# Routing done batch by batch, and half of the shared expert dealt between routed experts, in a cross-attention and mixture-of-experts layer

## The chip, the cores and the metric

The kernel runs on one core of a Trainium2 chip. The metric is the device time of one execution in microseconds (us). Before the change three runs gave 1760.06 us in the median (1760.02 to 1762.03). Everything below about single instructions comes from one further execution, which was profiled.

The engines are named as in the profile: PE is the matrix engine and PEld its weight loads, DVE the vector engine, ACT the scalar engine, POOL the general engine that also issues indirect DMAs, SP the engine that issues most other DMAs. Each runs its instructions in order.

## The reference

A layer of cross-attention, then a mixture-of-experts layer, on `x` of 4 batches of 512 tokens with 512 features; the context has 1601 rows a batch, of which the first 257 are an image and have weights of their own.

```python
h = x + xattn(layernorm(x), ctx)       # 16 heads of 32; softmax over text rows plus softmax over image rows
n = layernorm(h).reshape(T, 512)       # T = 2048 tokens
scores = sigmoid(n @ router_w.T)       # 32 experts in 8 groups of 4
sc = scores + e_bias
group = sum of the two largest sc of each group; keep the 3 best groups
topk_idx = 4 largest of the kept sc    # topk_w = their scores, normalised to sum 2.5
# capacity: each expert takes the first 80 tokens (in token order) that chose it
Y[e] = (silu(X[e] @ W_gate[e]) * (X[e] @ W_up[e])) @ W_down[e]      # X[e]: up to 80 x 512; I = 256
out = scatter_add(Y * w) + (silu(n @ shared_gate.T) * (n @ shared_up.T)) @ shared_down.T
return h + out
```

So one part of the result (the shared expert, hidden size 512) is computed for every token, and another (the routed experts) for 32 lists of at most 80 tokens. Both are added to `h`.

## The kernel before

**Attention.** A loop over the four batches `b` (line 517). It first projects keys: four blocks of context rows times four chunks of features, 16 calls of `keys` (line 595 on), and between these calls, from a hand-written table `side` (line 578), it runs norms (`take_norms`, `take_normed`) and the largest scores of the first head group (`scores`, lines 286 to 292, four PE matmuls into four banks and four DVE reductions). A hand-written list (line 601) follows, with the rest of these, values, and `residual` of the batch before (lines 421 to 457: output projection, `x1`, layer norm `xn`, transposed `xnT`, router logits). Then come four chunks of heads `c`, each a loop over 13 tiles `t` of keys (line 642): scores of the next chunk (`wave`, DVE reductions), exponentials on ACT (`exps`), weighted sums on PE, and sums of the exponentials (`added`) on POOL, in the last chunk on DVE.

PSUM has eight banks, which `psum` (line 123) hands out in turn; a new tile in a bank waits until the bank's last reader is done. `Later` (line 86) holds work that becomes due after so many steps.

Large SBUF tiles of 128 x 4 x 512 come from one pool of five buffers, `wide` (line 134): exponentials, weights and later the shared expert's input and hidden layer. After the last batch the first `xT` is loaded (line 711).

**Shared expert and routing.** `shared` (line 837) makes 48 units of work for the four batches: for each batch four `gate` and four `up` units (hidden chunks) and four `down` units (token tiles). Each is four matmuls of 128 x 128 by 512 in the program. A batch's downs are dealt between the next batch's gates; the downs of batch 3 come last. A down fetches the tile of `x1` from `x1_d` through SP, adds on DVE and stores to `out` through SP (lines 868 to 876).

The loop at line 977 issues the units one by one. At fixed units (8 and on) it puts in the residual work of batch 3, and after each unit as many routing steps as a budget allows (`SHARE`, `spent`). Routing (line 728) is a chain of small DVE operations: selection (scores, groups, four rounds of maximum), then a write of the weights into `xw_d` next to the normalised tokens, then `ranks` (PE transposes) and the search, in which DVE finds the 80 best-ranked tokens of every expert eight at a time (`max`, `match_replace`). It runs twice: `first` for batches 0 to 2 (12 tiles of 128 tokens) and `second` for batch 3. Weights of the first four experts are loaded at units 10, 14, 18 and 22. When all routing is issued, `tokens` (line 828) turns the result into token indices, with a PE transpose, and POOL gathers the rows of the first four experts.

**Routed experts.** A loop of 33 rounds (line 1003). Round `e` projects gate and up of expert `e`, has POOL gather rows for `e + 4`, transposes the rows of `e + 2`, and does the down projection of `e - 1`: ACT scales it into `y` (three buffers), and POOL issues an indirect DMA that adds `y` into rows of `out` (line 925). Then SP issues the weights of expert `e + 3`, 1.5 MB, into one of four sets of buffers. Each of these DMAs to `out` waits for the one before to land.

Of the kernel before, what the change touches and what calls it, by code (L numbers as in the profile page):

```python
# [80 lines left out]


# [25 lines left out]
def body(ctx, tc, a, ident, mhalf, logits, x1_d, xw_d, xnT_d, den_d, rec_d, out):  # L108
# [9 lines left out]
    pt, hold, row, st = pool("pt", 5), pool("hold", 4), pool("row", 5), pool("st", 3)  # L118
# [15 lines left out]
    def wide(name):  # L134
        return pt.tile([P, NC, 512], F32, name=name, tag="wide")
# [285 lines left out]
    def residual(b, qt, aoT, wo):  # L421
# [9 lines left out]
        def project_o():  # L431
            ps = psum()
            project(ps, lambda k: aoT[:, k, qt * P:(qt + 1) * P], lambda k: wo()[:, k, :])
            t["x1"] = rowt("x1")
            nc.vector.tensor_tensor(t["x1"], ps, t["xr"], ALU.add)
            nc.sync.dma_start(x1_d[rows, :], t["x1"])
            t["moments"] = moments(t["x1"])
# [21 lines left out]
    def queries(b, xs, n):  # L459

        qT = kv.tile([P, NC, L], F32, name="qT", bufs=2)
        xlT = kv.tile([P, NC, L], F32, name="xlT")
# [8 lines left out]
        return qT, sq, turn, [partial(part, c, at) for c in range(NC) for at in range(0, L, n)]  # L471

# [42 lines left out]
    nc.vector.tensor_tensor(v_b, v_b, vi_b, ALU.add)  # L515
    pending = []
    for b in range(B):
# [16 lines left out]
        sqs, rs = {"q": sq_q}, {}  # L534

# [59 lines left out]
        for bl in range(NB):  # L595
            for c in range(NC):
                keys(bl, c)
                for f in side.get((bl, c), ()):
                    f()
                later.step()  # L600
# [10 lines left out]
        for c in range(NC):  # L611
# [30 lines left out]
            for t in range(NKT):  # L642
# [32 lines left out]
                while t and done * (NKT - 1) < len(fill) * t:  # L675
                    fill[done]()
                    done += 1
                later.step()
                if more and t == NKT - 1:
                    part = parts[(c + 1) % 2]  # L680
                    split(mx, part, NM)
                if prepares:
# [28 lines left out]
    first_xT = wide("xT")  # L711
    nc.sync.dma_start(first_xT, xnT_d[:, :, :L])
# [11 lines left out]
    NR = NT - NQ  # L724
    SHARE = 2.3
    AHEAD = 4

    def routing(lo, n):


        tt, ts, tr = nc.vector.tensor_tensor, nc.vector.tensor_scalar, nc.vector.tensor_reduce

        def full(name):
            return rp.tile([P, NR, E], F32, name=name, tag=name)[:, :n, :]

        def small(name, k=1):
            return rp.tile([P, NR, k], F32, name=name, tag=name)[:, :n, :]

        def groups(name):
            return rp.tile([P, NR, NG, NG], F32, name=name, tag=name)[:, :n]  # L740

        lg = logits[:, lo:lo + n, :]
        sc, sb, cand, hit, sel, chosen = (full(x) for x in ("sc", "sb", "cand", "hit", "sel", "chosen"))
        m = [small(f"m{i}", NG) for i in range(4)]
        gs, rank, top = small("gs", NG), small("rank", NG), small("top")
        gt, eq = groups("gt"), groups("eq")
        g = sb.rearrange("p t (g k) -> p t g k", k=EG)
        one = gs.unsqueeze(3).to_broadcast([P, n, NG, NG])
        oth = gs.unsqueeze(2).to_broadcast([P, n, NG, NG])
        rv = rev.to_broadcast([P, n, E])  # L750
        before = below.unsqueeze(1).to_broadcast([P, n, NG, NG])

        def wide_(x):
            return x.to_broadcast([P, n, E])

        work = [
            lambda: nc.scalar.activation(sc, lg, AF.Sigmoid),
            lambda: tt(sb, sc, e_b.unsqueeze(1).to_broadcast([P, n, E]), ALU.add),

            lambda: tt(m[0], g[:, :, :, 0], g[:, :, :, 1], ALU.max),  # L760
            lambda: tt(m[1], g[:, :, :, 0], g[:, :, :, 1], ALU.min),
            lambda: tt(m[2], g[:, :, :, 2], g[:, :, :, 3], ALU.max),
            lambda: tt(m[3], g[:, :, :, 2], g[:, :, :, 3], ALU.min),
            lambda: tt(m[1], m[1], m[3], ALU.max),
            lambda: tt(m[3], m[0], m[2], ALU.min),
            lambda: tt(m[0], m[0], m[2], ALU.max),
            lambda: tt(m[1], m[1], m[3], ALU.max),
            lambda: tt(gs, m[0], m[1], ALU.add),

            lambda: tt(gt, oth, one, ALU.is_gt),  # L770
            lambda: tt(eq, oth, one, ALU.is_equal),
            lambda: tt(eq, eq, before, ALU.mult),
            lambda: tt(gt, gt, eq, ALU.add),
            lambda: tr(rank, gt, AX.X, ALU.add),
            lambda: ts(rank, rank, float(TKG), None, ALU.is_lt),
            lambda: tt(
                cand.rearrange("p t (g k) -> p t g k", k=EG), g, rank.unsqueeze(3).to_broadcast([P, n, NG, EG]), ALU.mult
            ),
        ]

        for k in range(TOPK):
            into = sel if k else chosen
            work += [
                lambda: tr(top[:, :, 0], cand, AX.X, ALU.max),
                lambda: tt(hit, cand, wide_(top), ALU.is_equal),
                lambda: tt(hit, hit, rv, ALU.mult),
                lambda: tr(top[:, :, 0], hit, AX.X, ALU.max),
                lambda into=into: tt(into, hit, wide_(top), ALU.is_equal),
            ]
            if k:  # L790
                work.append(lambda: tt(chosen, chosen, sel, ALU.add))
            if k < TOPK - 1:
# [258 lines left out]
```

## Time and profile before

| what | value |
|---|---|
| median of three runs | 1760.06 us |
| profiled execution, whole / its span | 1755.5 / 1753.8 us |
| mean clock granted to PE | 0.992 |
| PE, DVE, ACT, POOL busy | 1699.4, 954.3, 642.4, 866.2 us |
| attention ends and the shared expert begins on PE | 1344 us |
| first expert transpose on PE | 1534.9 us |
| last `y` on ACT, last scatter on POOL | 1738.2, 1746.3 us |
| weights of one matrix of an expert, issue to landing | 5.3 to 7.0 us (512 KB) |
| scatter `out<-y`, on POOL / issue to landing | 1.42 / 5.7 us (3.7 to 8.1) |
| gather `xp<-xw_d`, on POOL / issue to landing | 0.93 / 5.4 us (2.8 to 7.6) |

The page is read from the slices inwards: they cut the span in 40 equal parts, each digit being the busy share of an engine in tenths. Matmul ends are modelled, so that a full PE may still hide short waits. A line of the order of time gives start, duration, engine, source line, operation and tiles; in brackets stands how long the engine was idle before it and what ended the wait. In a list of waits the numbers are total us, times, and the longest.

### The profile page before, as it was taken

To read this page: it belongs to the slowest core of one execution; us is meant where nothing else is said; L and a number is where in the kernel's file an instruction comes from. 1 tells how busy PE (TensorE), PEld (TensorE's weight loads), DVE (VectorE), ACT (ScalarE), POOL (GpSimd) and SP (SyncE) were. 2 spreads that over 40 slices of the span, in tenths; PEclk is the share of its full clock that TensorE was granted. 3 is DMA by queue.
4 is the path that set the end of the run, shared out by engine and by line. 5 is a ranking of instruction groups with operands and counts; after the bars stand their busy time and mean duration, and the time that the engine had idled before them with its cause. 6 is when DMAs were issued, how large, how long until landed. Compare 5 with 4: busy or idle time off the path is not lost. (4 is left out here: it accounts for less than half of the span.)

```text
span 1753.8 us, 29354 instructions
## 1 busy us (share of the span) xinstructions
PE 1699.4 (97%) x11825; PEld 895.0 (51%) x11825; DVE 954.3 (54%) x1861; ACT 642.4 (37%) x1368; POOL 866.2 (49%) x612
## 2 busy tenths in 40 slices
PE   6999999999999999999999999999999999998896
PEld 3564444456544444564444445644442454486674
DVE  3675554757555556665555648555557767411110
ACT  2125456611355565114555631245556010011111
POOL 2327878332569753328679432388782300123332
PEclk9999999999999999999999999999999999999998
DMA  6000000311100004020000040300011453379994
GB/s 226 1 2 1 26 22 6 110 65 56 42 1 26 26 13 150 19 79 13 27 1 27 14 161 13 108 2 14 14 49 63 144 185 114 97 262 292 294 288 102
DMA packets 68455, 138.38 MB, mean 79 GB/s; under 512 B 16096, under 2 KB 28512, under 8 KB 66144
## 3 DMA queue, kind: packets, MB, share of 16 engines
q1 hardware_dynamic: 59984, 125.42, 21.0%
q0 software_dynamic: 5120, 10.82, 3.1%
q8 instruction: 93, 1.52, 0.4%
q10 hardware_dynamic: 3216, 0.28, 0.1%
q14 instruction: 42, 0.34, 0.1%
HBM read 113.68 MB, written 22.81 MB: 78 GB/s over the span
## 5 line engine op out<-in xcount | busy, mean ns | idle before, releaser
L356 ACT ACTIVATE pT<-ps 128x512 f32<-128x512 f32 (+1 forms) x832 | 429.4, 604 | 344.0 <-PE ps L355 333.6
L318 DVE TENSOR_REDUCE mx<-ps 128x1 f32<-128x512 f32 (+1 forms) x576 | 331.3, 617 | 289.0 <-PE ps L304 289.0
L371 POOL TENSOR_TENSOR acc<-acc,pT 128x1024 f32<-128x1024 f32 x192 | 445.6, 2363 | 3.0 <-ACT pT L356 2.7
L363 PE MATMUL po<-pT,v 128*32 128x512 f32 (+2 forms) x1792 | 222.2, 603 | 0.0
L274 PEld LDWEIGHTS ps<-v_w,cT 128*128 128x128 f32 (+1 forms) x1408 | 168.9, 186 | 102.2 <-DVE mx L318 56.1
L355 PE MATMUL ps<-qT,kT 32*128 32x512 f32 (+1 forms) x1664 | 214.0, 587 | 0.0
L304 PE MATMUL ps<-kT,qT 32*128 32x512 f32 (+1 forms) x1536 | 205.2, 549 | 0.0
L274 PE MATMUL ps<-v_w,cT 128*128 128x128 f32 (+1 forms) x1408 | 197.7, 284 | 0.0
L213 PE MATMUL ps<-cT,wk 128*128 128x512 f32 (+1 forms) x384 | 153.9, 546 | 0.0
L292 DVE TENSOR_REDUCE mx<-ps 128x1 f32<-128x512 f32 (+2 forms) x256 | 128.4, 566 | 7.2 <-PE ps L289 7.2
L925 POOL DMA_INDIRECT out<-y,tok x32 | 45.4, 1419 | 140.8 <-DMA out<-y,tok 73.7
L220 POOL TENSOR_TENSOR sq_k<-sq_k,sq 128x512 f32<-128x512 f32 (+2 forms) x48 | 49.5, 1031 | 115.0 <-ACT sq L217 115.0
L352 PEld LDWEIGHTS <-pick 32*128 32x128 bf16 (+1 forms) x832 | 21.6, 91 | 165.7 <-issue 164.0
L213 PEld LDWEIGHTS ps<-cT,wk 128*128 128x128 f32 x384 | 69.6, 190 | 70.5 <-issue 54.3
L282 ACT COPY v<-ps 128x128 f32<-128x128 f32 (+1 forms) x208 | 60.1, 289 | 118.4 <-PE ps L274 117.8
L378 POOL TENSOR_TENSOR acc<-pT 128x1024 f32<-128x1024 f32 x24 | 56.1, 2359 | 86.7 <-ACT pT L356 54.1
L371 DVE TENSOR_TENSOR acc<-acc,pT 128x1024 f32<-128x1024 f32 (+1 forms) x72 | 97.8, 1405 | 2.1 <-ACT pT L356 2.1
L915 DVE TENSOR_TENSOR ehT<-ehT,ps 128x160 f32<-128x160 f32 x32 | 10.3, 321 | 162.0 <-ACT ehT L914 162.0
L371 POOL TENSOR_TENSOR pT<-pT 65x1024 f32<-65x1024 f32 x24 | 56.0, 2349 | 85.8 <-PE po L363 77.3
L304 PEld LDWEIGHTS ps<-kT,qT 32*128 32x128 f32 x1536 | 81.0, 183 | 30.8 <-issue 10.1
L363 PEld LDWEIGHTS po<-pT,v 128*32 128x32 f32 (+2 forms) x1792 | 34.7, 107 | 118.8 <-issue 109.3
L890 POOL DMA_INDIRECT xp<-xw_d,tok x32 | 30.0, 937 | 120.3 <-DVE tok L835 110.8
(178 smaller groups left out, 2233.8 us busy)
## 6 DMA issues: line engine op xcount, KB each, us to landing
W_gate<-in_W_gate SPq DMA_DIRECT2D x32, 512.0 KB, 5.6
W_up<-in_W_up SPq DMA_DIRECT2D x32, 512.0 KB, 7.0
W_down<-in_W_down SPq DMA_DIRECT2D x32, 512.0 KB, 5.3
xt<-in_x SPq DMA_DIRECT2D x32, 256.0 KB, 3.5
cT<-in_ctxT SPq DMA_DIRECT2D x8, 1024.0 KB, 9.4
rb<-rec_d SPq DMA_DIRECT2D x64, 128.0 KB, 2.7
wk<-in_k_w SPq DMA_DIRECT2D x4, 1024.0 KB
wki<-in_k_img_w SPq DMA_DIRECT2D x4, 1024.0 KB, 10.5
```

What stands on the lines that cost most here:

```text
L213: nc.tensor.matmul(ps[:, :n], lhsT=wt[:, k, c * P:(c + 1) * P], rhs=xT[:, k, to], start=k == 0, stop=k == NC - 1)
L220: nc.gpsimd.tensor_tensor(sq[:, to], sq[:, to], s, ALU.add)
L274: nc.tensor.matmul(ps[lo:hi, :], lhsT=cTs[bl][:, k, at:at + hi - lo], rhs=ws[bl == NB - 1][:, k, c * P:(c + 1) * P], start=k == 0, stop=k ...
L282: nc.scalar.copy(v[:n, t, :], ps[:n])
L292: nc.vector.tensor_reduce(mx[:, qt, g, bl:bl + 1], ps[:, :n], AX.X, ALU.max, negate=True)
L304: nc.tensor.matmul(ps[:, j * n:(j + 1) * n], lhsT=qT[r:r + HD, c, q * P:(q + 1) * P], rhs=kT[r:r + HD, c, k0:k0 + n], start=True, stop=True,)
L318: nc.vector.tensor_reduce(mx[:, qt, g, i:i + 1], ps[:, :m], AX.X, ALU.max, negate=True)
L355: nc.tensor.matmul(ps[:n], lhsT=kT[r:r + HD, c, t * P:t * P + n], rhs=qT[r:r + HD, c, :], start=False, stop=True)
L356: nc.scalar.activation(pT[:n, g, :], ps[:n], AF.Exp)
L363: nc.tensor.matmul(po[r:r + HD, :], lhsT=v[rows, t, r:r + HD], rhs=pT[rows, g, :], start=start, stop=stop)
L371: (nc.vector if idle else nc.gpsimd).tensor_tensor(to[rows, h, :], to[rows, h, :], pT[rows, h, :], ALU.add)
L378: (nc.vector if idle else nc.gpsimd).tensor_tensor(acc[:, h, :], pTs[0][:, h, :], pTs[1][:, h, :], ALU.add)
```

## The change

- `wide` deals its five buffers out by hand (a list `wides`), so that one can be kept back. The first `xT` is loaded in the middle of the last chunk of batch 3 into a buffer that is kept until the shared expert of batch 0 has used it.
- Routing is by batch, four tiles at a time. Its scratch space is one tile, cut into pieces; selection and search are two lists. For batches 0 and 1 it runs in attention of batches 2 and 3: four selection steps after each call of `keys`, and one search step after each tile of the head chunks but the last. The best 80 so far (`best`) are merged with each batch's 512 tokens, so each search scans 592 values. For batches 2 and 3 it runs in the loop of shared units as before.
- The shared expert's 48 units become two lists: 24 for batches 0 and 1, issued as before, and 24 for batches 2 and 3 (`BEFORE = 2`), dealt over the first rounds of the routed experts. For batches 2 and 3 `residual` writes `x1` straight to `out`; their `down` units fetch nothing: ACT copies the product out of PSUM and POOL issues a DMA that adds it into `out`.
- In the loop of shared units: residual work of batch 3 begins at unit 5; `SHARE` is 2.9 with other costs per step; `later.step` is called twice per unit; weights are loaded at units 3, 6, 9, 12 and 15 for five experts; all routing, `tokens` and the first gathers are issued before the last two units.
- Expert weights have five sets of buffers instead of four, and are issued for `e + 4`.

```diff
-    def wide(name):
-        return pt.tile([P, NC, 512], F32, name=name, tag="wide")
+    wides = list(range(5))
+
+    def wide(name, keep=False):
+
+        n = wides.pop(0)
+        t = pt.tile([P, NC, 512], F32, name=name, tag=f"wide{n}")
+        if keep:
+            return t, n
+        wides.append(n)
+        return t
...
-            nc.sync.dma_start(x1_d[rows, :], t["x1"])
+
+            nc.sync.dma_start((x1_d if b < BEFORE else out)[rows, :], t["x1"])
...
+        work += [
+            lambda: nc.gpsimd.iota(
+                key, [[-1, L]], base=T - b * L, channel_multiplier=0, allow_small_or_imprecise_dtypes=True
+            ),
+            lambda: nc.vector.tensor_copy(merged[:, :CAP], best),
+            ranks,
+        ]
+        search = []
+        for j in range(CAP // 8):
+            at = best[:, 8 * j:8 * j + 8]
+            search.append(lambda at=at: nc.vector.max(at, merged))
+            if j < CAP // 8 - 1:
+                search.append(lambda at=at: nc.vector.match_replace(merged, at, merged, 0.0))
+        return work, search
...
+        if b > 1:
+            space = kv.tile([P, NC, L], F32, name="space", tag="xlT")
+            select, search = routing(b - 2, space.rearrange("p c t -> p (c t)"))
...
                 keys(bl, c)
                 for f in side.get((bl, c), ()):
                     f()
+                for f in select[:4]:
+                    f()
+                del select[:4]
                 later.step()
...
+                if b == B - 1 and not more and t == NKT // 2:
+                    first_xT = wide("xT", True)
+                    nc.sync.dma_start(first_xT[0], xnT_d[:, :, :L])
                 later.step()
...
+                if more and t and search:
+                    search.pop(0)()
...
             def down(j, n=n, t=t, fetch=fetch):
...
                 ps = psum()
                 project(ps, lambda k: t["hT"][:, k, j * P:(j + 1) * P], lambda k: sd[:, k, :])
-                nc.vector.tensor_tensor(t[j], t[j], ps, ALU.add)
-                nc.sync.dma_start(out[n * L + j * P:n * L + (j + 1) * P, :], t[j])
-
+                if n < BEFORE:
+                    nc.vector.tensor_tensor(t[j], t[j], ps, ALU.add)
+                    nc.sync.dma_start(out[rows, :], t[j])
+                else:
+                    y = held("ys")
+                    nc.scalar.copy(y, ps)
+                    nc.gpsimd.dma_start(out[rows, :], y, accum_op=ALU.add)
...
-    wgp = pool("wgp", 4, side="right", reuse_waits="tile")
+    wgp = pool("wgp", 5, side="right", reuse_waits="tile")
...
+    first, second = (
+        select + search
+        for select, search in (routing(b, rp.tile([P, 1024], F32, name=f"space{b}")) for b in (B - 2, B - 1))
+    )
+    O_AT = 5
...
+    ready = O_AT + NQ + 3
+    LAST = len(units) - 2
     spent = 0.0
     for i, u in enumerate(units):
         if i < 2:
             continue
+        if i == LAST:
+            for f in first + second:
+                f()
+            tokens()
+            for e in range(AHEAD):
+                gather(e)
         u()
         for f in side.get(i, ()):
             f()
         later.step()
...
+        later.step()
+
+        if i == ready + 1:
+            spent = (i - 2) * SHARE
+        while spent < (i - 1) * SHARE and (first or i > ready and second):
+            todo = first or second
+            spent += 0.67 if len(todo) < 2 * CAP // 8 else 0.23
             todo.pop(0)()
...
+        if i % 3 == 0 and i // 3 - 1 < 5:
+            weights[i // 3 - 1] = expert_weights(i // 3 - 1)
     turn(0)
     turn(1)
+    n_between, done = len(between), 0
     for e in range(E + 1):
...
         if e:
             down(e - 1)
-            if e + 3 < E:
-                weights[e + 3] = expert_weights(e + 3)
-
+            if e + 4 < E:
+                weights[e + 4] = expert_weights(e + 4)
+        while done < n_between and done * (E - 5) < n_between * (e + 1):
+            between.pop(0)()
+            done += 1
```

## The prediction

> **What bounds the kernel now.** I read the page's slices first, then busy time by stretch, then the order of time on PE, ACT, DVE and POOL around the last 400 us. The slices:
>
> ```profile
> span 1753.8 us, 29354 instructions
> PE   6999999999999999999999999999999999998896
> DMA  6000000311100004020000040300011453379994
> GB/s 226 1 2 1 26 22 6 110 65 56 42 1 26 26 13 150 19 79 13 27 1 27 14 161 13 108 2 14 14 49 63 144 185 114 97 262 292 294 288 102
> ```
>
> PE is full until about 1535 us; only the last five slices, the routed experts, show gaps in PE, and there DMA is at 9 tenths. The stretches (PE, PEld, DVE, ACT, POOL busy, clock, DMA share, GB/s):
>
> ```profile
> 1344.00:1536.00 192.00, 190.03 (x513) 86.62 (x513) 124.77 (x218) 21.88 (x33) 22.34 (x25) 1.00 0.39 127
> 1536.00:1741.00 205.00, 187.06 (x1273) 146.28 (x1272) 24.22 (x65) 31.54 (x64) 66.85 (x56) 0.96 0.85 263
> 1058.00:1090.00 32.00, 32.00 (x179) 19.64 (x176) 30.61 (x52) 4.30 (x10) 9.76 (x14) 1.00 0.03 9
> ```
>
> The shared expert (first row) is PE work from end to end; the routed experts (second) leave PE idle or half clocked; and in the later half of batch 3's key projections (third) DVE is busy 30.6 of 32 us beside a full PE. ACT's order of time gives the price of the expert stage: y is written once per expert.
>
> ```profile
> 1546.35 0.68 ACT L924 ACTIVATE y<-ps,xp 80x512 f32<-80x512 f32 x1 [1.70 <-PE ps L920]
> 1551.88 0.68 ACT L924 ACTIVATE y<-ps,xp 80x512 f32<-80x512 f32 x1 [1.70 <-PE ps L920]
> ...
> 1641.39 0.30 ACT L914 ACTIVATE ehT<-ps 128x160 f32<-128x160 f32 x1 [2.80 <-PE ps L207]
> 1647.62 0.68 ACT L924 ACTIVATE y<-ps,xp 80x512 f32<-80x512 f32 x1 [5.92 <-PE ps L920]
> ...
> 1736.52 0.68 ACT L924 ACTIVATE y<-ps,xp 80x512 f32<-80x512 f32 x1 [1.47 <-PE ps L920]
> 1738.23 0.68 ACT L924 ACTIVATE y<-ps,xp 80x512 f32<-80x512 f32 x1 [1.03 <-PE ps L920]
> ```
>
> An undisturbed round is 5.53 us (1551.88 less 1546.35). 30 of them and the last 1.7 are 167.6; the stage took 1738.2 - 1546.35 = 191.9. So **24.3 us are waits**, with the clock they cost. The waits in that stage name their source:
>
> ```profile
> POOL out L925 <- DMA out<-y,tok: 73.7, 18, 6.3
> PE ps L901 <- DMA xp<-xw_d,tok: 14.0, 9, 2.6
> ```
>
> Each scatter waits on POOL for the landing of the one before; the gathers stand behind it in the same queue, and PE's transposes wait for them. At the end, without load, scatters still come 4.7 us apart and two are late:
>
> ```profile
> 1741.61 1.39 POOL L925 DMA_INDIRECT out<-y,tok  x1 [3.11 <-DMA out<-y,tok]
> 1746.30 1.39 POOL L925 DMA_INDIRECT out<-y,tok  x1 [3.30 <-issue]
> ```
>
> The price of a shared-expert unit is PE's cadence, 1509.59 - 1506.15 = 3.43 us for eight matmul records:
>
> ```profile
> 1506.15 3.60 PE L207 MATMUL ps<-xT,shared_gate 128*128 128x512 f32 x8
> 1509.59 3.60 PE L207 MATMUL ps<-xT,shared_up 128*128 128x512 f32 x8
> ```
>
> **What the Trainium skill says.** "TensorE: Matmul & The Clock Gate", Part 1, What's actually happening: a PE idle for about a window of 3.4 us falls to half its clock and needs about 3.4 us of work to return. The trace agrees on the half: after the wait at 1641.4 the four L920 records take 3.33 us, elsewhere 1.88; here the idle was only 2.3 us. "DMA: Bandwidth & Descriptors", SWDGE vs HWDGE vs iDMA: a DMA that accumulates must be issued by GpSimd, so the new adds share POOL's queue with gathers and scatters; no direct one is in this trace. Same page, Anatomy of one DMA: about 2.0 us plus bytes over 436e3, which estimates 2.6 us for 256 KB; the scatter of 160 KB takes 3.3 us to land when unloaded, so I take the page as a lower end. "VectorE: DVE Perf Modes", The TRN2 errata: every vector instruction carries a fixed cost, so small ones are dear. The trace agrees: 384 elements take 0.56 us, 128 take 0.29.
>
> **The change part by part**, against the profiled execution (1755.5 us, span 1753.8).
>
> 1. Shared expert of batches 2 and 3 (24 units, 82.3 us of PE) leaves the shared stage and is dealt into rounds 0 to 25, one a round. PE's work is the same; its place changes. A round becomes 5.53 + 3.43 = 8.96 us. What set the stalls then has time: weights and rows of one expert, 1.57 + 0.34 MB, need 5.9 us at the 324 GB/s seen with all DMA engines busy; a scatter 4.7 to 6.5. The last six rounds are bare, 5.53 us, with weights fetched by then (five buffers, issued four rounds ahead). Removed: 24.3. I keep 2 for leftovers (0 to 8: the first rounds, and switches of PE between shapes).
>
> 2. Accumulating DMAs, eight, on POOL, each waiting for the last scatter and delaying the next one. Queued behind them: gathers due two rounds later, so a delay of one round is covered. Price, not in the trace: issue 1.4 (as a scatter), landing 2.6 (the page) to 8.1 (slowest scatter landing); taken 3.8 and 0.3 between, 5.5. With a scatter at 5.4 a round with an add needs 10.9 against 8.96. The last four adds fall into rounds 22 to 25: 7.8 us behind; six bare rounds win back about 3. Scatter 31 then comes 8.7 us after y 31; before, 8.1. Tail: +0.5 (-4 to +8). The DVE adds and fetches of x1r and the plain stores that go were covered by PE.
>
> 3. Routing of batches 2 and 3 stays in the shared stage, now with 24 units of cover instead of 48. PE there: 24 x 3.43 = 82.3; four output projections 13.7; logits, turns, the attention's last heads and rank transposes 9.0: 105.0. From 1344.1 the first expert transpose could come at 1449.1. Before it came at 1534.9, which less 82.3 is 1452.6. So -3.5. But DVE: one batch of four tiles was routed after 1471.5, and without the shared expert's interleaved work it took 14.7 us to select and 15.4 to search. Batch 3's logits are there when unit 12 is done: 1344.1 + 13 x 3.43 + 22.2 = 1410.9. DVE gets to it after unit 13's product, at 1415; 30.1, the new copy of `best` 0.2, and six products and sums of the shared expert at 0.6 in between give 1449; `past` 0.4 more. PE arrives at the token transpose after unit 21 at 1410.9 + 9 x 3.43 + 0.5 = 1442.3 and waits about **7.2 us** (3 to 9), then runs some 3.4 us at half clock: +1.7. Two units (6.9 us) follow and cover the gathers, which need about 6. In all -3.5 + 7.2 + 1.7 = +5.4, with the token transpose +5.6. Behind the waiting PE stand only those units; nothing else is late.
>
> 4. Routing of batches 0 and 1 inside attention of 2 and 3. The search is one op a tile (0.77 or 0.83 us), queued on DVE behind its reductions, where DVE idles 2.04 us before the next four: nothing. The 54 selection steps go four to a key chunk, chunks 0 to 13. To chunk 6 DVE is idle more than half: nothing. From chunk 7 (1058 on) 7.7 us of DVE work (20 at 0.32 less the short ones, rank product 0.67) enter a DVE that has about 1.1 us to give. PE writes a bank that DVE must have emptied eight tiles earlier; this ring lets PE lead by some 5 us and 3 were in use (scores of block 1 end on PE at 1083.9, on DVE at 1086.9). Walking the ring tile by tile, PE ends the scores of block 2, tile 1 at 1094.4 instead of 1088.6: 5.8 us a batch (4.6 if all lead is used, 7.7 if none), plus 0.45 for rank transposes that PE now does here. Batch 2 shows the same DVE load at 725 to 750. Two batches: **+12.5** (5 to 16).
>
> 5. At nothing: the first xT load moved into the last chunk (PE had no gap for it at 1344; four rotating pT buffers are enough because DVE had finished each tile's add 4 us before the fourth-next exp), output projections three units earlier (aoT was ready at 1372.9; they now start at 1371.5, and the scaling is called a unit earlier; if not, 1.5 us), weights from unit 3 on (127 GB/s in that stage), constants at the start.
>
> Sum: -24.3 + 2 + 0.5 + 5.6 + 12.5 = -3.7, so 1751.8 for such an execution. The median of the runs shown is 1760.06, 4.6 above the profiled one; I take the difference over: **1756**.
>
> **Rivals.** A difference below 0.2%, 3.5 us, can't be told from none.
> - *The sum* (0.46): own range 1749 to 1762, faster in somewhat over half of it, no change in a third.
> - *DVE's work finds cover* (0.30): the key chunks cost 2 us a batch because the early ring slack is larger than I walked, and tokens wait 4 without losing the clock. -24.3 + 1 + 0 + 0.5 + 4.9 = -17.9: 1742. For it: DVE is idle 17 us in chunks 0 to 6. Against: 30.6 of 32 us busy later.
> - *The key projections take selection at full price* (0.18), slower: 14.7 + 0.45 us a batch is the most, 30.3 against 12.5. Halfway, 21.4, gives +5.2: 1765; all of it 1774. It cancels the gain from 16.2 us on and is slower by 0.2% from 19.7, 9.9 a batch. For it: these are chains of dependent small ops between which the norm copies of the next block wait. Against: DVE is idle early.
> - *The adds take over as the bound* (0.06), slower: landing at 8.1 makes a round 15.2, four of them 25 us late, 22 after recovery; the tail grows by about 17: 1772. Against: no DMA load of 9 tenths remains in those rounds. That the experts stay bound by scatters, so that nothing is filled, is not so otherwise: 32 x 6.4 + 8 x 5.5 = 249 is below PE's 261.
>
> Faster: 0.25 + 0.30 = 0.55; same 0.15; slower 0.06 + 0.18 + 0.06 = 0.30. For eight in ten: 1741 to 1768.
>
> **What would show it.** Right: y's at 8.96 us with PE full and clock 1.00 until round 25, then 5.53; a wait of PE's token transpose on DVE's `past` near 7 us; key chunks of batches 2 and 3 about 6 us longer each, PE's weight loads waiting on DVE reductions or selection; DVE reductions of the tile loop as before. Wrong: rounds longer than 9 us or POOL's adds landing over 6 us; key chunks unchanged (then near 1742) or 10 us longer (then slower).

## The result, and the profile after

The changed kernel takes 1770.93 us in the median of five runs (1767.00 to 1772.71) against 1760.06 (1759.15 to 1762.03) for the kernel before: a ratio of 1.0055, 95% interval 1.0040 to 1.0071. It is slower by about 11 us. The forecast was 1756, range 1741 to 1768; time and direction were both wrong. The profiled execution took 1771.67 us (span 1769.9), 16.1 of span more than the one before. The tables below account for these 16.1; the medians lie only 10.9 apart, because the execution profiled before was 4.6 us faster than its median and this one 0.7 slower than its own.

From the page of the changed kernel, the span and three rows of its 40 slices:

```profile
span 1769.9 us, 29516 instructions
...
PE   6999999999999999999999999999999998999996
...
DMA  6000000212100004020000040300011564767773
GB/s 224 1 2 1 26 26 1 109 64 65 32 2 26 26 14 147 20 78 13 26 1 26 14 159 14 108 2 14 14 49 62 177 219 127 240 222 229 223 217 58
```

The row of nines for DMA has gone: the weights now spread over a longer stage (7 tenths, 220 GB/s where it was 290). PE looks full. The time shows only in the stretches, cut at the beginning of the shared expert, the first expert transpose, the first and the last `y` (columns as before: the window and its us; PE, PEld, DVE, ACT and POOL busy; clock, DMA share, GB/s):

```profile
1358.00:1480.50 122.50, 110.14 (x310) 49.79 (x307) 83.56 (x201) 17.10 (x25) 19.73 (x27) 0.96 0.48 161
...
1495.00:1755.00 260.00, 251.52 (x1380) 170.53 (x1378) 26.63 (x66) 39.16 (x77) 75.39 (x64) 0.97 0.70 208
```

| stretch | before | after | change | forecast |
|---|---|---|---|---|
| to the beginning of the shared expert | 1344.1 | 1358.0 | +13.9 | +12.5 |
| to the first expert transpose, 82.3 us of PE work taken out | 108.5 | 122.5 | +14.0 | +5.6 |
| to the first `y`, with one unit (3.4) now in it | 11.5 | 14.5 | +3.0 | +3.4 |
| to the last `y`, 78.9 of PE work put in | 191.9 | 260.0 | -10.8 net of it | -22.3 |
| after the last `y` | 15.6 | 14.9 | -0.7 | +0.5 |

(24 units, 82.3 us of PE work, were moved: one of them, 3.4, counts in the third row, the other 23, 78.9, in the fourth. The forecast's -24.3 + 2 stands in the fourth.) Two rows are wrong: the shared stage by 8.4 us and the experts by 11.5.

The order of time on ACT shows both kinds of round. First the early ones, then the end:

```profile
1503.90 0.68 ACT L991 ACTIVATE y<-ps,xp 80x512 f32<-80x512 f32 x1 [1.69 <-PE ps L987]
1512.87 0.68 ACT L991 ACTIVATE y<-ps,xp 80x512 f32<-80x512 f32 x1 [1.69 <-PE ps L987]
...
1718.22 0.68 ACT L991 ACTIVATE y<-ps,xp 80x512 f32<-80x512 f32 x1 [1.74 <-PE ps L987]
1730.26 0.68 ACT L991 ACTIVATE y<-ps,xp 80x512 f32<-80x512 f32 x1 [8.25 <-PE ps L987]
```

1512.87 less 1503.90 is 8.97: the filled round is what it was taken for. The bare round from 1718.22 takes 12.04 instead of 5.53. PE's order of time says why:

```profile
1719.72 1.95 PE L217 MATMUL ps<-xpT,W_up 128*128 128x80 f32 x16
1725.99 0.77 PE L968 MATMUL ps<-ident,xp 80*128 80x80 f32 x4 [4.33 <-DMA xp<-xw_d,tok]
1726.55 3.62 PE L987 MATMUL ps<-W_down,ehT 128*80 128x512 f32 x4
```

PE waits 4.33 us for gathered rows and then runs at half its clock (3.62 for what takes 1.88). And POOL's order of time says why the rows are late (L992 scatter, L938 add, L957 gather):

```profile
1683.33 1.42 POOL L992 DMA_INDIRECT out<-y,tok  x1 [5.86 <-ACT y L991]
1690.76 0.95 POOL L938 DMA_DIRECT2D out<-ys  x1 [6.01 <-issue]
1692.02 0.99 POOL L957 DMA_INDIRECT xp<-xw_d,tok  x1 [0.30 <-issue]
1697.73 1.48 POOL L992 DMA_INDIRECT out<-y,tok  x1 [4.72 <-issue]
1702.11 0.93 POOL L938 DMA_DIRECT2D out<-ys  x1 [2.90 <-DMA out<-y,tok]
...
1709.19 1.47 POOL L992 DMA_INDIRECT out<-y,tok  x1 [4.85 <-DMA out<-ys]
1717.63 0.93 POOL L938 DMA_DIRECT2D out<-ys  x1 [6.97 <-issue]
1718.86 0.99 POOL L957 DMA_INDIRECT xp<-xw_d,tok  x1 [0.30 <-issue]
...
1733.61 1.47 POOL L992 DMA_INDIRECT out<-y,tok  x1 [2.57 <-DMA out<-ys]
```

Each add waits on POOL until the scatter before it has landed, and each scatter until the add has; the gather stands behind the add. Where the bracket names a DMA, it is such a landing (2.90 for the add at 1702.11, 4.85 and 2.57 for scatters). For the two longest waits of adds (6.01, 6.97) the profile names nothing (`issue`); that they are of the same kind is shown by experiment 2, where they go with the order. The gather at 1718.86, whose rows PE wanted at 1721.66 and got at 1725.99, would have stood at 1702.97 in step, that is with nothing late and no add before it (1683.33 plus two rounds of 8.96, and 1.72 from a scatter to its gather): 15.9 late. Four rounds with an add, 1683.33 to 1733.61, took 12.57 us each.

The lag of POOL's scatter behind its own `y` on ACT, expert by expert (us, from the two orders of time; a scatter in step has 1.0), is the reading that explains the stage. The kernel without the adds comes from the first experiment below.

```
expert          10   11   12   13   14   15   16   17   18   19   20   21   22   23   24   25   26   27   28   29   30   31
after          1.0  6.3  9.0  8.4  7.5 10.3 15.9 15.2  8.7  5.7  1.4  0.9  6.4  8.9 15.0 15.4  8.1  5.9  5.0  4.4  3.8  6.8
without adds   1.0  1.0  1.0  1.0  1.0  1.0  1.0  3.4  1.0  1.0  1.0  1.0  1.0  1.0  1.0  1.0  2.9  2.1  1.2  0.9  0.9  3.9
```

Four adds put the chain of DMAs to `out` some 15 us behind, twice; it falls from 15.2 to 8.7 and from 15.4 to 8.1 also because PE has been made to wait.

In the shared stage, PE's list of waits (total us, times, longest; the first line belongs to the experts):

```profile
PE ps L968 <- DMA xp<-xw_d,tok: 8.4, 3, 4.3
PE ps L886 <- DVE past L884: 5.9, 1, 5.9
PE ps L596 <- DVE space L575: 3.4, 2, 2.4
PE ps L458 <- DVE xn L212: 3.1, 2, 1.8
```

The token transpose (L886) waits less than forecast (5.9, not 7.2). The two below it, rank transposes (L596) and transposes of `xn` (L458), were not in the forecast. DVE's order of time shows where it came late:

```profile
1420.75 0.77 DVE L609 MAX8 best<-merged 32x8 f32<-32x592 f32 x1
1425.25 0.69 DVE L933 TENSOR_TENSOR x1r<-x1r,ps 128x512 f32<-128x512 f32 x1 [3.73 <-DMA x1r<-x_d]
...
1433.19 0.19 DVE L466 COPY logits<-ps 128x32 f32<-128x32 f32 x1 [4.47 <-PE ps L217]
1436.77 0.69 DVE L915 TENSOR_TENSOR hT<-hT,ps 128x512 f32<-128x512 f32 x1 [3.39 <-PE ps L217]
1437.38 0.28 DVE L542 TENSOR_TENSOR space<-space,e_b 128x128 f32<-128x128 f32 x1
```

At 1425 an add of the shared expert holds DVE 3.73 us for a fetch that SP issued only at 1418.85, behind three weight DMAs. Then batch 2's search is done, and DVE idles until 1436.77, although batch 3's logits had been copied by 1433.4: the loop admits the second routing only after the next unit (`i > ready`), whose product is the line at 1436.77.

### The profile page after: what moved, and what is told of

Its sections match the earlier page's. It is cut to its first block, busy times and chain, and to the rows that moved or that the text cites. A ratio compares the mean times of both kernels' runs of the same rounds, so it can differ in the third digit from the quotient of the medians.

```text
span 1769.9 us, 29516 instructions
## 1 busy us (share of the span) xinstructions
PE 1711.9 (97%) x11825; PEld 900.5 (51%) x11825; DVE 975.6 (55%) x2012; ACT 653.4 (37%) x1382; POOL 871.5 (49%) x622
## 5 line engine op out<-in xcount | busy, mean ns | idle before, releaser
L223 PE MATMUL ps<-cT,wk 128*128 128x512 f32 (+1 forms) x384 | 153.9, 546 | 0.0
L992 POOL DMA_INDIRECT out<-y,tok x32 | 45.9, 1434 | 160.2 <-ACT y L991 80.7
L982 DVE TENSOR_TENSOR ehT<-ehT,ps 128x160 f32<-128x160 f32 x32 | 10.3, 321 | 195.9 <-ACT ehT L981 195.9
L223 PEld LDWEIGHTS ps<-cT,wk 128*128 128x128 f32 x384 | 69.6, 190 | 70.5 <-issue 52.8
L314 PEld LDWEIGHTS ps<-kT,qT 32*128 32x128 f32 x1536 | 82.0, 183 | 30.8 <-issue 10.1
L362 PE MATMUL ps<-mT,pick 32*128 32x512 bf16 (+1 forms) x832 | 83.3, 387 | 5.2 <-ACT pT L366 2.8
```

Source lines behind the costliest of these rows:

```text
L223: nc.tensor.matmul(ps[:, :n], lhsT=wt[:, k, c * P:(c + 1) * P], rhs=xT[:, k, to], start=k == 0, stop=k == NC - 1)
L314: nc.tensor.matmul(ps[:, j * n:(j + 1) * n], lhsT=qT[r:r + HD, c, q * P:(q + 1) * P], rhs=kT[r:r + HD, c, k0:k0 + n], start=True, stop=True,)
L362: nc.tensor.matmul(ps[:n], lhsT=pick[r:r + HD, kind(t), :n], rhs=mT[r:r + HD, :], start=True, stop=False)
```

## The experiments

Four theories were tried. *The adds* (A): they cost the expert stage, through their place in the order of DMAs to `out` (A1) or through issue and traffic (A2). *DVE's idle time* in the shared stage makes PE wait (F). *Selection* in the later key chunks (D) costs what the forecast said. *The fifth buffer* (W): it alone removed the waits that the kernel before had, and the dealing adds nothing. Ratios are to runs of the kernel before on the same chip; its medians there were 1758.9 to 1760.6.

**1. No adds.** The eight DMAs are left out, and with them that part of the result.

```diff
                     nc.scalar.copy(y, ps)
-                    nc.gpsimd.dma_start(out[rows, :], y, accum_op=ALU.add)
```

> The changed kernel without the eight DMAs that add the shared expert of batches 2 and 3 into out (the products are computed and copied, but that part is missing from the result). Theory A: the adds hold up POOL's queue, gathers come late behind them, and this makes most of the 13.5 us of waits among the experts. Then the three waits of PE's transposes for gathered rows (8.4 us, and the half clock after them) go, the time from the first y to the last falls from 260.0 to about 248, and the median from 1771 to about 1760. Rival B: the waits come from DMA load by weights and rows, not from the order on POOL. Then the span from first to last y stays above 256 and the median above 1767. Nothing before the experts changes under either.

1752.66 us, ratio 0.9958 (0.9944 to 0.9973): 18 us less than the change. First to last `y`, the stretch of the experts:

```profile
1493.80:1740.00 246.20, 246.00 (x1381) 168.15 (x1379) 26.33 (x66) 39.23 (x77) 67.59 (x57) 1.00 0.68 212
```

PE is busy 246.00 of 246.20 us at full clock: every wait of the stage is gone, those of the kernel before included. After the last `y` come 11.4 us instead of 14.9. The adds cost 14.0 + 3.5 = 17.5 us.

**2. The same adds to another tensor.** `x1` of batches 2 and 3 and the adds go to `x1_d`, so that both are missing from the result; issue, traffic and copies stay, the order with the scatters goes.

```diff
-            nc.sync.dma_start((x1_d if b < BEFORE else out)[rows, :], t["x1"])
+            nc.sync.dma_start(x1_d[rows, :], t["x1"])
...
-                    nc.gpsimd.dma_start(out[rows, :], y, accum_op=ALU.add)
+                    nc.gpsimd.dma_start(x1_d[rows, :], y, accum_op=ALU.add)
```

> The changed kernel with the eight adds of the shared expert, and x1 of batches 2 and 3 that they add to, going to x1_d instead of out (so that these parts are missing from the result). Same DMAs on the same queue with the same bytes; what is gone is the order between them and the scatters into out. Theory A1 (order): an add costs because it waits for the scatter before it to land and the next scatter waits for the add, on one queue with the gathers behind. Then this runs like the kernel without adds: first to last y 246 to 250, tail from the last y 11 to 12.5 us, median within 4 us of 1753. Theory A2 (traffic and issue): read-modify-write traffic or the issue on POOL costs: first to last y 255 or more, median 1766 or more.

1754.61 us, 0.9963 (0.9951 to 0.9976); first to last `y` 246.0 again. POOL's order of time in this kernel:

```profile
1705.74 1.48 POOL L992 DMA_INDIRECT out<-y,tok  x1 [3.43 <-ACT y L991]
1709.04 0.93 POOL L938 DMA_DIRECT2D x_d<-ys  x1 [1.83 <-ACT ys L937]
1710.28 1.00 POOL L957 DMA_INDIRECT xp<-xw_d,tok  x1 [0.30 <-issue]
1714.70 1.47 POOL L992 DMA_INDIRECT out<-y,tok  x1 [3.42 <-ACT y L991]
```

The scatters are 8.96 us apart with the add between them. So A1: the order costs the time; the DMAs themselves cost nothing in this stage that can be seen.

**3. One add a batch.** The four tiles of a batch are collected and added by one DMA of 1 MB.

```diff
-                    y = held("ys")
-                    nc.scalar.copy(y, ps)
-                    nc.gpsimd.dma_start(out[rows, :], y, accum_op=ALU.add)
+                    if j == 0:
+                        t["ys"] = wide("ys")
+                    nc.scalar.copy(t["ys"][:, j, :], ps)
+                    if j == NQ - 1:
+                        rows = out[n * L:(n + 1) * L, :].rearrange("(j p) d -> p j d", p=P)
+                        nc.gpsimd.dma_start(rows, t["ys"], accum_op=ALU.add)
```

> The four tiles of a batch's shared expert are collected in one 128 x 4 x 512 tile and added into the output by one DMA of 1 MB, so there are two adds instead of eight; bytes and order are the same. If the cost of the adds is their number (each takes a place in the chain in which every DMA to the output waits for the landing of the one before), most of the 17.5 us that dropping them gave comes back: each of the two may take 8 to 10 us of the chain instead of four times 5 to 6, so the chain needs 32 x 5.5 + 2 x 9 = 194 us against 246 us of PE work, with one late gather or none; first to last y 248 to 251 us and a time of 1754 to 1760. If the cost is bytes or POOL's descriptors, nothing is won: 1768 to 1773.

1771.97 us, 1.0073 (1.0053 to 1.0093): nothing won, and my expectation of 8 to 10 us for such an add was wrong. The group of these adds, its last line the time from issue to landing:

```profile
L941 POOL DMA_DIRECT2D out<-ys x2: 1384/1390/1397, 1637.4 to 1719.0; - x2
...
DMA to landing us min/median/max: 14.0/14.5/15.0
```

The eight adds of the change have 4.0/6.2/6.5 there. Three times as many bytes on top cost 8.3 us, so about 95 GB/s (786 KB in 8.3 us; an estimate from these two sizes, and 76 to 103 with the medians of 4.2 to 6.9 us that the small adds have in the other kernels with this order), where weights and rows were seen at 324 in the kernel before (1550 to 1570 us). One add of 1 MB holds the chain as long as four adds put it behind: the scatter after it lags by 15.5 and 13.6 us, against 15.9 and 15.4.

**4. Gathers one round earlier.** If late gathers alone were the harm, this would cure it.

```diff
-    AHEAD = 4
+    AHEAD = 5
...
-            xps[e] = ew.tile([CAP, D + E], F32, name="xp", bufs=6)
+            xps[e] = ew.tile([CAP, D + E], F32, name="xp", bufs=7)
```

> The changed kernel with gathers issued five experts ahead instead of four, and seven buffers for the rows instead of six. The adds stay. Theory A (gathers late behind adds): one more round of lead, 9 us, covers most of the lateness of up to 14 us; the waits of PE for rows fall from 8.4 to under 3 us, first to last y to about 250, the median to about 1761. Rival C: the chain of adds and scatters itself is too long, and ACT's y then waits for its buffers instead: first to last y stays at 257 or more, with waits of ACT y on out<-y. Rival B (DMA load) expects no change either, but with the waits still on gathered rows.

1772.37 us, 1.0069 (1.0047 to 1.0091). The cover did what it should in the middle: there PE no longer waits, and expert 25's `y` comes 217.23 us after the first as without the adds (217.22; 223.28 in the change). But the chain does not go faster: the lag grows to 18.1 at expert 17 and 23.1 at expert 25, the last scatter is issued at 1762.87 against 1761.77, and PE meets the same end (rows waits 7.1 us, and ACT waits for a free `y` buffer). From 1624.5 us on both kernels' scatters need the same time to the end, 138.3 and 137.3: the chain is the bound, and the gathers only show it.

**5. Batch 3's routing a unit earlier, and its first fetch two units earlier** (F).

```diff
-        if i == ready + 1:
+        if i == ready:
             spent = (i - 2) * SHARE
-        while spent < (i - 1) * SHARE and (first or i > ready and second):
+        while spent < (i - 1) * SHARE and (first or i >= ready and second):
...
+        before = [None]
         for n in range(B):
             t = {}
 
-            def gate(ic, n=n, t=t):
+            def gate(ic, n=n, t=t, prev=before[0]):
                 if ic == 0:
                     t["hT"] = wide("hT")
+                    if prev and n < BEFORE:
+                        prev(0)
...
+            before[0] = fetch
+
...
-                    if j == 0:
-                        fetch(0)
+                    if j not in t:
+                        fetch(j)
```

> The changed kernel with two gaps of DVE in the shared stage closed: routing of batch 3 is issued from the unit after which its logits are there (unit 12) and not from the next one, and the first x1 row tile of batch 0 is fetched two units earlier, before expert weights in SP's queue. Theory F (DVE's routing is what PE waits for, at full length): DVE idled 3.7 us for the row tile and about 8 us between the batches' routing; with 6 to 10 us of it won, PE's wait at the token transpose (5.9) goes to 0 to 2 and the half clock after it too; the first expert transpose comes 6 to 10 us earlier after the stage's start than the 122.5 us before; median about 1763. Rival G (DVE has slack, PE waits for other reasons): the stage keeps 120 us or more.

1762.05 us, 1.0017 (1.0003 to 1.0030). The stage takes 115.3 us instead of 122.5, and the token transpose waits 1.3 instead of 5.9. DVE's order of time:

```profile
1423.51 0.69 DVE L938 TENSOR_TENSOR x1r<-x1r,ps 128x512 f32<-128x512 f32 x1 [1.86 <-DMA x1r<-x_d]
...
1428.42 0.29 DVE L542 TENSOR_TENSOR space<-space,e_b 128x128 f32<-128x128 f32 x1 [1.25 <-ACT space L541]
```

Selection of batch 3 begins at 1428.42, 73.1 us into the stage (1355.3); in the change 79.4. F holds: idle time of DVE, no lack of its speed, made most of that stage's excess over the forecast. The two edits were not tried apart.

**6. Eight selection steps after each key chunk**: the 54 steps end in chunk 6, where DVE has room.

```diff
-                for f in select[:4]:
+                for f in select[:8]:
                     f()
-                del select[:4]
+                del select[:8]
```

> The changed kernel with eight selection steps after each key chunk instead of four, so that they end by chunk 6, where DVE is idle more than half of the time. Theory D: only the steps in the later chunks cost, because DVE is full there. Then the 10.3 us that attention lost (scores of batch 3's last block ending at 1127.3 instead of 1115.9, less 1 us from the start) fall to about 2, and the median to about 1763. Rival E: any step put between key chunks costs PE about the same, by delaying norm copies and banks: still 8 us or more lost, median 1769 or more.

1768.73 us, 1.0062 (1.0040 to 1.0084), not to be told from the change. Its profiled execution (1761.68, the fastest of six) has the last of the largest-score reductions of batch 3 at 1122.6 instead of 1128.7, so the place was right; 2.1 us came back as waits for keys on DVE. In the median the gain stays within the spread of the runs. It shows better across the traces: the shared stage begins at 1350.7 to 1352.8 us in the four kernels with eight steps a chunk (this one and those of experiment 9) and at 1355.2 to 1358.6 in the eight with four.

**7. Selection moved into the head chunks**, four steps a tile, with the search behind it: the other place with idle DVE time.

```diff
-                for f in select[:4]:
-                    f()
-                del select[:4]
...
-                if more and t and search:
-                    search.pop(0)()
+                if more and t:
+                    for f in select[:4] or search[:1]:
+                        f()
+                    if select:
+                        del select[:4]
+                    else:
+                        del search[:1]
```

> The changed kernel with the selection of batches 0 and 1 taken out of the key projections and put, four steps a tile, into the loop over key tiles of the first two head chunks, ahead of the search, where DVE idles 2 us a tile. Theory D2: what attention lost (10.3 us; 5 to 6 with eight steps a chunk) was DVE standing between PE and its banks in the key projections; in the tile loop 1.3 us a tile fit into the gap. Then the scores of batch 3's last block end within 1.5 us of before plus the start's 1 us, the tile loops grow by less than 2 us in all, and the shared stage begins at 1346 to 1349 instead of 1358 (1355 to 1358 in other runs); median about 1761. Rival E2: the tile loop has no real slack either, and the loss returns there: shared stage at 1353 or later.

1811.71 us, 1.0295 (1.0270 to 1.0320): a clear miss. DVE's order of time in this kernel, then POOL's over the same stretch:

```profile
819.56 2.46 DVE L556 TENSOR_TENSOR space<-space,below 128x256 f32<-128x256 f32 x1
822.06 2.44 DVE L557 TENSOR_TENSOR space<-space 128x256 f32<-128x256 f32 x1
824.54 0.42 DVE L558 TENSOR_REDUCE space<-space 128x32 f32<-128x256 f32 x1
...
840.06 0.29 DVE L571 TENSOR_REDUCE space<-space 128x4 f32<-128x128 f32 x1
```

```profile
814.58 9.64 POOL L381 TENSOR_TENSOR acc<-acc,pT 128x1024 f32<-128x1024 f32 x4 [3.86 <-ACT pT L366]
...
839.89 9.38 POOL L381 TENSOR_TENSOR acc<-acc,pT 128x1024 f32<-128x1024 f32 x4 [0.90 <-ACT pT L366]
```

The operation of L557 takes 0.42 us in the shared stage of the changed kernel (at 1441.19). Here it takes 2.44, about as long as one of POOL's four sums (9.64 / 4 = 2.41). Taking the four as equal, the third ends at 821.81 and the fourth at 824.22; L556 ends at 822.02 and L557 at 824.50. The same holds for every selection step of these two head chunks and of the next batch's that has two inputs and begins within a sum: it ends within 0.3 us of the end of that sum. A reduction is not held: the one at 840.06 begins within a sum that lasts to 842.2 and takes its usual 0.29. (The reduction at 824.54 begins when POOL's sums are over.) The reductions of scores stand behind the held steps, and PE behind them. Its waits from 640 to 1390 us:

```profile
PE ps L362 <- DVE mx L330: 15.0, 4, 4.3
PE ps L362 <- DVE mx L328: 9.0, 4, 3.6
```

These 24.0 us are absent in the change; its shared stage begins at 1358.0, here at 1389.3.

**8. Fewer batches dealt.** `BEFORE = 3` deals one batch (12 units, 4 adds), `BEFORE = 4`, with batch 3's downs in the first list, none.

```diff
-BEFORE = 2
+BEFORE = 3
```

> The changed kernel with the shared expert of one batch instead of two dealt among the experts (12 units, four adds), and 36 units in the loop that covers routing. Theory F: in the shared stage PE waits for DVE's routing (17.5 us with the half clock that follows, against 105.0 of PE work); with 41 us more cover the wait at the token transpose goes, and most of the rest: the stage takes 146.2 us of PE work plus at most 5. Among the experts the mean round is 5.53 plus 1.3; waits there between 5 and 14 us. Sum: 12 to 17 us less than the changed kernel's 1771, so 1754 to 1759. Rival G: the waits in that stage come from late x1r loads and half clocks and not from too little cover: the stage keeps 12 us or more of waits, median 1766 or more.

1766.35 us, 1.0041 (1.0027 to 1.0055), where 1754 to 1759 was expected. The shared stage takes 156.3 us, 10.1 more than PE's work: the token wait nearly goes with the cover (1.1 us), the waits for ranks and `xn` stay (3.5 and 2.3). Among the experts 223.4 us pass from first to last `y`, 18 more than the work (167.6 and 11 units); PE still waits 10.7 us for rows.

```diff
-BEFORE = 2
+BEFORE = 4
...
-        units[1] += downs
+        units[0] += downs
```

> The changed kernel with nothing dealt: all 48 units in the shared stage, x1 through x1_d, no adds; routing by batch, two batches inside attention, five weight buffers stay. Cover for routing is now ample: the stage takes 187.3 us of PE work and at most 4 of waits. If five buffers don't matter, experts wait as before the change: first to last y 192 (24.3 of waits). Then the median is that of before plus attention's 10, less 3: 1765 to 1770. If the fifth set of weight buffers takes waits away (theory W): first to last y 180 or less, median 1757 or less. With the chain of scatters as the cause (theory A) it is the former.

1777.24 us, 1.0076 (1.0051 to 1.0100), where 1765 to 1770 was expected: 199.6 us from first to last `y`, so 32 of waits where the kernel before has 24 (the profiled execution was the slowest of six). The shared stage keeps 11.4 us over PE's 187.3 instead of at most 4, though the token wait is 1.1. W falls: a fifth set of weight buffers did not take the waits of bare rounds away. The dealing does: with it and without adds (experiment 1) none is left.

**9. Repairs together.** Experiments 5 and 6 in one kernel; the same with one add a batch; the same with `BEFORE = 3`. The edits are those above.

> Both repairs that won something alone: eight selection steps after each key chunk instead of four, and batch 3's routing and the first x1r fetch taken one step earlier in the shared stage. The adds are as in the change. If the two are independent their gains add: 8.7 us in the median from the second and 2 to 6 from the first, 1756 to 1760. If the earlier selection only moves the waits (the new ones for kT on DVE), 1760 to 1764.

> Both repairs and the two large adds in place of eight. If the three losses found (order of adds, DVE's idle time in the shared stage, selection in the later key chunks) are separate, 1771 - 8.7 - 4 - 13 = 1745, with first to last y near 249 us and the shared stage near 116 us; that is faster than both kernels. If they share waits, 1750 to 1756.

> Both repairs (eight selection steps a key chunk; batch 3's routing and the first x1r fetch one step earlier), and only batch 3's shared expert dealt among the routed experts (12 units and 4 adds of 256 KB). Four of the eight adds go, but half of the rounds are bare and bound by weights and scatters again, where the same size without the repairs still lost 10.8 us to waits. If the repairs keep their worth beside the size: 1766.4 - 8.7 - 3 = 1755; as the token wait was only 1.1 us there, the second repair may be worth no more than 4, which gives 1759. Against the same two repairs with 24 units (1756.65) it is a tie in either case; a time under 1752 would say that the dealt batches are what costs.

| kernel | median | ratio to before | first to last `y` |
|---|---|---|---|
| both repairs | 1756.65 | 0.9991 (0.9977 to 1.0005) | 258.4 |
| and one add a batch | 1756.39 | 0.9977 (0.9968 to 0.9986) | 260.4 |
| and one batch dealt | 1760.09 | 1.0006 (0.9997 to 1.0014) | 222.1, with 12 units (41.2) less in it |

The two repairs together bring 14 us in the median (11 by the ratios); experiment 5 alone brought 9 (7 by the ratios). The expected 1745 for the second was too low by 11, for the reason of experiment 3; large adds bring nothing over small ones that can be told. It is the one version with the whole result whose interval lies below both the kernel before and the change, by 0.2% of the first. What is left in it is the chain: without the order the experts would need about 246 us (as in experiments 1 and 2), not 260. A version that keeps batches 2 and 3 dealt and needs no add into `out` was not made.

## Why the prediction was wrong

*Removed waits (step 1): right.* Filled rounds take 8.97 us, and without the adds (experiment 1) nothing is left of the 24.3 us of waits; the 2 us of leftovers were not needed.

*Adds (step 2): the step that failed.* It said of an add: "Queued behind them: gathers due two rounds later, so a delay of one round is covered", and priced it at 5.5 us, so that a round with an add needed 10.9 us of the chain of DMAs to `out`. Three things were wrong in it. A gather behind an add is held twice: by what the chain is late already, and by the add's own wait for the scatter before it (6 to 7 us); together 15.9 in the case shown. An add takes 6.2 us from issue to landing, and a scatter 6.4 (both medians in the changed kernel), so that the round was 12.57. And I applied the lag only to the last four adds, not to the four in the middle. The middle four cost 6.06 us of PE time (expert 19 to 25 against the kernel without adds), by one late gather and the half clock after it. The last four put the chain 14.4 us behind (4 times 12.57 - 8.96) where I had 7.8; of these 3.6 were won back in the bare rounds (I had 3), 10.8 stayed. 6.1 + 10.8 = 16.9 of the 17.5 measured. In the forecast the same adds cost 4.8 and vanished in a tail that was no longer than before. Both signs of being wrong that it named for this step came: rounds over 9 us, and adds landing after more than 6. The rival "the adds take over as the bound" had the right mechanism and its size (17), but put it into the tail, where the runs have 14.0 of 17.5 among the experts; it got 6% because I took a landing of 8.1 as needed for it and looked only at the load on the DMA engines, while experiment 2 shows no part of the load in it. That its 1772 lies beside the measured 1770.93 is in part luck: it had the shared stage 8.4 us too short, and the profiled executions lie 5 us further apart than the medians.

*Routing in the shared stage (step 3): right mechanism, mis-sized.* Waits of PE in the stage are 122.5 - 105.0 = 17.5 us where I had 9. The token wait was smaller than forecast (5.9), its half clock as forecast (+1.7). Missing were the rank transposes (3.4), those of `xn` (3.1) and a second spell at half clock (1.7); under 2 us lie in small pieces. DVE's own path was right: from the first selection step (1437.38) to the end of the search (1471.4) 34.0 us, where the forecast has 33.9. It began late. I had batch 3's selection begin after unit 13's product, as it did, but 71 us into the stage; it was 79, because PE had lost most of these 8 us by then, waiting for a DVE that selected, searched and was held by a fetch behind weights on SP. I had walked DVE's path to the token transpose, and not what DVE owed PE on the way. The two things that experiment 5 changes stood in the diff, and took 7.2 us of the 8.4 back.

*Attention (step 4): right.* +10.3 us at the last reductions of batch 3 (5.4 and 4.9 a batch, from the two orders of time) against 12.5, and by the mechanism named: PE's weight loads wait longer there on DVE's score reductions (in batch 3's stretch, 970 to 1135 us, 3.0 us at L223 and 2.4 at L299, before 0.8 and 1.2). Search in the head chunks cost about 0.3. The rest of the +13.9 is 1.0 at the start and 2.2 at half clock after a wait of 2.8 us for ACT in the last chunk, which the kernel before has too, there without the loss; in other runs of these kernels it comes and goes, so I lay no weight on it.

*Tail (in step 2) and the edits at nothing (step 5):* as forecast, the tail only by luck: without adds it is 11.4 us, so the adds cost 3.5 there where they were given 0.5.

In sum: +1.4 attention, +8.4 shared stage, -0.4 and -1.2 around the experts, +11.5 in them, is 19.7 of the 19.8 between -3.7 and +16.1.

## What to carry to other kernels

In these kernels the DMAs that add into one tensor ran one after the other. Where a trace shows that, count the landing times, not the issue, and walk that chain through the whole stage: here its lag added up over neighbouring adds, to 15 us, and a load queued behind a waiting add took the lag and that wait as well (15.9). When work is moved as cover, ask what it brings along; here the cover came with its own writes to the tensor that was already the bound. And before a stage is called bound by an engine, look whether that engine was let at its work: one unit in a condition and one load behind three others on a queue were together worth 7 us.

## What the runs showed of the hardware

- An accumulating DMA of 256 KB from POOL took 6.2 us from issue to landing in the median of the changed kernel (4.2 in experiment 4, 6.9 with both repairs), one of 1 MB 14.5. Only experiment 3 shows how landing grows with bytes; landing of the 256 KB adds apart from the scatters (experiment 2) was 4.8 in the median.
- DVE operations with two inputs in SBUF took up to 2.46 us instead of 0.42 beside POOL's sums (experiment 7): begun within a sum, they ended with it, while a reduction kept its 0.29. The Trainium skill, "SBUF — State Buffer", Who interferes with whom, says that a DVE instruction with two SBUF inputs contends with a GpSimd instruction that reads SBUF. The trace agrees, and puts the price at up to one POOL operation (2.4 us) each.
- PE fell to half its clock after waits of 3.25 and 4.33 us, but a wait of 2.8 us did so in one profile and not in another. In the changed kernel's shared stage a wait of 1.77 us was followed by half clock (0.50 from 1428 to 1430; 5.29 us for what takes 3.60), one of 2.41 us was not. The length of a wait alone does not settle it here; what does is open.

```profile
1391.37 0.61 PE L596 MATMUL ps<-ident,space 128*32 128x128 f32 x4 [2.41 <-DVE space L575]
1391.82 3.60 PE L217 MATMUL ps<-xT,shared_up 128*128 128x512 f32 x8
...
1426.55 0.66 PE L458 MATMUL ps<-ident,xn 128*128 128x128 f32 x4 [1.77 <-DVE xn L212]
1427.04 5.29 PE L217 MATMUL ps<-xT,shared_gate 128*128 128x512 f32 x8
```
